# A second level of Strassen for layer 0 of a two-layer graph network, with a new order rule for VectorE and GpSimd

## The chip, the core and the metric

The kernel runs on one core of one Trainium2 chip. The time is the device time of one execution in microseconds (us), and a figure for a kernel is the median of its executions. Kernels are compared by their ratio to the kernel before.

Engines in the profile: PE is TensorE's matmuls, PEld its weight loads, DVE VectorE, ACT ScalarE, POOL GpSimd, SP the queue that issues transfers.

## The reference

```
x: 128 graphs x 128 nodes x 512 features; adj: 128 x 128 x 128; all float32
# layer 0
deg = sum(adj, -1);  agg = (adj @ x) / max(deg, 1e-6)
u = layernorm(x + relu(concat[x, agg] @ W0.T))
# layer 1: three graph convolutions
h1 = relu(adj @ (u @ W1) + b1);  h2 = relu(adj @ (h1 @ W2) + b2)
out = layernorm(u + adj @ (h2 @ W3) + b3)
```

Layer 0 is computed as x @ Wa + (adj / deg) @ (x @ Wb). So there are five weight products (y = x Wb, l0 = x Wa, and h1, s2, s3) and four adjacency products.

## The kernel before

Four graphs are one quad, and there are 32 quads. A weight product is a 512x512 by 512x512 product cut into 2x2 blocks of 256x256, and Strassen's method in Winograd's form makes it seven block products in place of eight. One block product is four matmuls of 128x128 weights by 256 columns:

```python
def product(p, a, b, k, start, transposed):
    (ta, ka), (tb, kb) = a.block(k), b.block(k)
    def emit():
        for o in range(2):
            for c in range(2):
                ...                                   # lhsT 128x128, rhs 128x256
                pinned(nc.tensor.matmul(bank_ap(p)[:, o, :], lhsT, rhs, start=..., stop=c == 1))
    plan.op("PE", 1.728, emit, ka + kb, [p])
```

Partial sums stay in a PSUM bank as long as possible. Where an intermediate sum is wanted, ScalarE copies the bank to SBUF and TensorE adds the next product to the same bank (`py` below):

```python
def wino_a(key, a, b, c00, c11, transposed=False, inner=None):
    py, pz, px = Slot("bank"), Slot("bank"), Slot("bank")
    product(py, a, b, 1, True, transposed)
    s1 = copied(py)                                   # ScalarE: bank -> SBUF
    product(pz, a, b, 5, True, transposed)
    product(py, a, b, 6, False, transposed)           # adds to py once s1 is taken
    s2 = copied(py)
    product(px, a, b, 2, True, transposed)
    ...
```

The sums of blocks that Strassen wants are made by GpSimd for the data and by VectorE for the weights (once). Each quad's degrees are summed by VectorE, inverted, written to HBM and read back so that every partition has the row:

```python
def degrees(q):                       # abridged
    vector(..., nc.vector.tensor_reduce(d, AR_T[q % 2], axis=AX.X, op=OP.add))   # "deg"
    ...
    dma(dd <- d)       # 2 KB, element by element
    dma(R_T <- dd)     # read back as a row for all partitions
```

All instructions are first put into a plan. A small list scheduler with a duration for each operation fixes the order of every engine before anything is emitted; TensorE may take an operation from up to `AHEAD = 24` places further on if the first one is not ready. Two quads are always in flight: layer 0 and h1 of one, and s2, h2, s3 and the last product of the one before it.

## Time and profile before

| | before |
|---|---|
| median time | 2423.27 us (2419.84 to 2429.75, 4 runs) |
| profiled span | 2426.3 us |
| TensorE busy | 2390.6 us, 11776 records |
| VectorE / ScalarE / GpSimd busy | 864.1 / 800.6 / 895.2 us |

TensorE is the bound, without a hole in whole periods. The prediction below shows the lines, so only the reading is given here: look first at the share of TensorE in the span and in the chain that ended last, then at the periods, and only then at its few waits. A busy engine's mean duration is not its pace, because matmuls are pipelined; the pace is the distance between starts.

### The profile page before, as it was taken

How to read it: one execution, taken by the hardware profiler on the slowest of the kernel's cores; microseconds unless marked ns; L12 is line 12 of the kernel's file. 1: busy time of each engine (PE TensorE's matmuls, PEld its weight loads, DVE VectorE, ACT ScalarE, POOL GpSimd, SP SyncE). 2: the span in 40 equal slices, each digit the busy share in tenths (PEclk: the TensorE clock that was granted, in tenths of full speed). 3: DMA queues.
4: the chain of work that ended last, by engine and by line, in shares of the span. 5: the costliest groups of instructions: out<-in, count | busy, mean ns of one | idle time of the engine just before them, and what ended most of it. 6: DMA issues, size and time to landing. Idle time of an engine off the chain costs nothing.

```text
span 2426.3 us, 29271 instructions
## 1 busy us (share of the span) xinstructions
PE 2390.6 (99%) x11776; PEld 2079.8 (86%) x11776; DVE 864.1 (36%) x1685; ACT 800.6 (33%) x1345; POOL 895.2 (37%) x772
## 2 busy tenths in 40 slices
PE   7999999999999999999999999999999999999997
PEld 6888888888888888888888888888888888888886
DVE  5433332333333333332343333333323433233323
ACT  2233333233332333233333333333233333333333
POOL 3333433334333344332443333433334432344323
PEclk9999999999999999999999999999999999999999
DMA  8201211112111121110111111211111111011100
GB/s 208 57 30 63 66 49 57 44 48 65 53 56 48 40 65 57 53 61 27 65 57 53 61 41 51 66 57 53 51 37 61 53 48 61 22 61 55 42 18 35
DMA packets 56360, 133.30 MB, mean 55 GB/s; under 512 B 21920, under 2 KB 27040, under 8 KB 48160
## 3 DMA queue, kind: packets, MB, share of 16 engines
q1 hardware_dynamic: 55552, 131.16, 16.9%
q8 instruction: 93, 1.52, 0.3%
q14 instruction: 43, 0.35, 0.1%
q10 hardware_dynamic: 672, 0.26, 0.1%
HBM read 97.78 MB, written 33.62 MB: 54 GB/s over the span
## 4 chain that ended last, share of the span: by engine, by line
PE 95%; DMA 3%; DVE 1%; issue 0%; ACT 0%; SPq 0%; POOL 0%; ACTq 0%; POOLq 0%; DVEq 0%
PE bank L408 77%; PE bank L646 5%; PE bank L687 5%; PE bank L421 4%; PE bank L563 4%; DMA dd<-deg 2%; DMA r<-dd 1%; DMA xT<-in_xT_dram 0%; DVE st L489 0%; SPq L265 0%; DVE deg L374 0%; DVE ah L275 0%; DVE row L275 0%; DVE deg L375 0%; ACT s L394 0%
## 5 line engine op out<-in xcount | busy, mean ns | idle before, releaser
L273 POOL TENSOR_TENSOR T<-T 128x512 f32<-128x512 f32 x384 | 484.9, 1274 | 1225.0 <-ACT T L656 970.1
L408 PE MATMUL bank<-w,T 128*128 128x256 f32 x3584 | 800.1, 379 | 2.3 <-ACT s L394 2.3
L408 PEld LDWEIGHTS bank<-w,T 128*128 128x128 f32 x3584 | 675.9, 190 | 92.8 <-ACT s L394 2.3
L394 ACT COPY s<-bank 128x512 f32<-128x512 f32 x480 | 281.3, 586 | 1225.5 <-PE bank L408 1225.2
L275 DVE TENSOR_TENSOR row<-bank,s 128x512 f32<-128x512 f32 x288 | 198.8, 691 | 690.5 <-PE bank L408 545.3
L408 PE MATMUL bank<-wb,xT 128*128 128x256 f32 x1792 | 404.5, 380 | 6.0 <-DMA wb<-in_w0T_dram 5.6
L408 PEld LDWEIGHTS bank<-T,w 128*128 128x128 f32 x1792 | 340.3, 190 | 74.5 <-issue 31.3
L408 PE MATMUL bank<-T,w 128*128 128x256 f32 x1792 | 397.8, 379 | 1.5 <-issue 1.5
L408 PE MATMUL bank<-wa,xT 128*128 128x256 f32 x1792 | 397.7, 379 | 0.0
L408 PEld LDWEIGHTS bank<-wb,xT 128*128 128x128 f32 x1792 | 341.5, 191 | 53.3 <-issue 5.6
L408 PEld LDWEIGHTS bank<-wa,xT 128*128 128x128 f32 x1792 | 340.5, 190 | 46.3
L273 POOL TENSOR_TENSOR u<-u,b 128x512 f32<-128x512 f32 x128 | 164.3, 1285 | 188.0 <-PE bank L563 186.4
L273 POOL TENSOR_TENSOR xT<-xT 128x512 f32<-128x512 f32 x128 | 163.8, 1280 | 61.6 <-DMA xT<-in_xT_dram 49.4
L563 PEld LDWEIGHTS bank<-at,u 128*128 128x128 f32 x1024 | 130.9, 195 | 12.4 <-ACT u L506 6.8
L563 PE MATMUL bank<-at,u 128*128 128x128 f32 x1024 | 132.3, 279 | 6.4 <-ACT u L506 6.4
L275 DVE TENSOR_TENSOR bank<-bank,s 128x512 f32<-128x512 f32 x96 | 67.2, 700 | 195.3 <-PE bank L421 195.3
L421 PE MATMUL bank<-row,ah 128*128 128x256 f32 x512 | 126.2, 379 | 2.3 <-DVE ah L275 2.3
L687 PE MATMUL bank<-row,at 128*128 128x512 f32 x256 | 120.5, 594 | 5.6 <-DVE row L275 5.6
L646 PEld LDWEIGHTS bank<-at,row 128*128 128x128 f32 x1024 | 119.4, 192 | 1.7
L530 DVE SCALAR_TENSOR_TENSOR u<-bank,x 128x512 f32<-128x512 f32 x128 | 88.3, 690 | 89.7 <-PE bank L421 87.5
L590 ACT ACTIVATE T<-T,b 128x256 f32<-128x256 f32 x192 | 90.5, 503 | 89.0 <-DVE T L275 89.0
L646 PE MATMUL bank<-at,row 128*128 128x128 f32 x1024 | 119.5, 275 | 0.0
(30 smaller groups left out, 1226.1 us busy)
## 6 DMA issues: line engine op xcount, KB each, us to landing
x<-in_x_dram SPq DMA_DIRECT2D x32, 1024.0 KB, 6.5
out_dram<-o SPq DMA_DIRECT2D x64, 512.0 KB, 2.6
xT<-in_xT_dram SPq DMA_DIRECT2D x31, 1024.0 KB, 4.8
ar<-in_adj_dram SPq DMA_DIRECT2D x32, 256.0 KB, 2.8
at<-in_adjT_dram SPq DMA_DIRECT2D x32, 256.0 KB, 2.6
r<-dd SPq DMA_DIRECT2D x31, 256.0 KB, 4.5
w<-in_w_dram SPq DMA_DIRECT2D x12, 256.0 KB, 10.1
xT<-in_xT_dram SPq DMA_DIRECT2D x4, 256.0 KB, 5.0
```

What stands on the lines that cost most here:

```text
L273: gpsimd(n, lambda: pinned(nc.gpsimd.tensor_tensor(dst(), a(), b(), op=op)), reads, writes)
L275: vector(n, lambda: pinned(nc.vector.tensor_tensor(dst(), a(), b(), op=op)), reads, writes, shared)
L394: scalar(512, lambda: pinned(nc.scalar.copy(S_T[s.index], bank_ap(p))), [p], [s])
L408: nc.tensor.matmul(bank_ap(p)[:, o, :], lhsT, rhs, start=start and o == 0 and c == 0, stop=c == 1, skip_group_check=True,)
L421: nc.tensor.matmul(bank_ap(p)[:, j, :], AH_T[:, g, :], y.t[:, g, h * H : (h + 1) * H], start=False, stop=True, skip_group_check=True,)
L530: nc.vector.scalar_tensor_tensor(u.ap(m, h), bank_ap(p), 0.0, X.ap(m, h), op0=OP.max, op1=OP.add)
L563: nc.tensor.matmul(bank_ap(p)[:, c // 2, (c % 2) * P : (c % 2 + 1) * P], u.t[:, g, c * P : (c + 1) * P], a[:, g, :], start=True, stop=True ...
L590: lambda t=t, o=o: pinned(nc.scalar.activation(t, t, AF.Relu, bias=B1_T[:, 2 * h + o : 2 * h + o + 1])),
L646: nc.tensor.matmul(bank_ap(p)[:, g // 2, (g % 2) * P : (g % 2 + 1) * P], s.t[:, g, o * P : (o + 1) * P], a[:, g, :], start=True, stop=True ...
L687: nc.tensor.matmul(bank_ap(p).rearrange("p a n -> p (a n)"), a[:, g, :], s.t[:, g, :], start=True, stop=True, skip_group_check=True,)
```

## The change

The intent: in y and l0, all quads but the first cut each of the seven 256x256 block products again, into seven products of 128x128 blocks. That makes 49 matmuls of 128 columns where 28 of 256 columns stood. It needs inner sums of the weights (once) and of xT (each quad). The first four outer products are summed before the last three are added. Around it, the scheduler's rules change: VectorE may take a sum planned for GpSimd when that sum is urgent (`HELP`), the search ahead is longer, and a GpSimd instruction that is planned behind a VectorE instruction on their common port waits for it by semaphore (`behind`). The deadlines of the work behind TensorE are reckoned anew (`HOLD`). Buffers are rearranged to make room, the degree row is loaded straight into the tile of the scaled adjacency, and s3's end has an order of its own. Smaller parts ride along: the adjacency is loaded and its degrees summed at another place in the plan, xT is loaded and the output stored in twice as many transfers, and the layer norm's epsilon is added on GpSimd.

The diff, cut to its core ("..." marks cuts):

```diff
-    AHEAD = 24
+    AHEAD, HELP, HOLD = 32, 8.0, 8.0
...
             if o.shared:
-                port = (o.engine, end)
+                if o.engine == "POOL" and port[0] == "DVE":
+                    o.behind = port[2]
+                port = (o.engine, end, o)
...
+                if e == "DVE":
+                    can += [
+                        o for o in known["POOL"]
+                        if o.other and ready_at[o] <= t and o.latest + slip < t + self.HELP and has_room(o, t)
+                        and port_free(e, t)
+                    ]
...
+    def inner_product(p, a, b, ps, i, start):
+        parts = [(a.inner(k, i), b.inner(k, i)) for k in ps]
+        def emit():
+            for n, ((ta, _), (tb, _)) in enumerate(parts):
+                pinned(nc.tensor.matmul(quarters(p, 4)[:, n], ta, tb, ...))      # 128 columns each
+        plan.op("PE", 0.222 * len(ps), emit, ...)
+
+    def outer_a(key, a, b, c11):              # outer products 1, 7, 6, 5: batch of four
+        inner_product(py, a, b, BATCH[0], 1, True)
+        s1 = copied(py)
+        inner_product(pz, a, b, BATCH[0], 5, True)
+        inner_product(py, a, b, BATCH[0], 6, False)
+        ...
+        add("POOL", F, outer(2), outer(2), outer(0), ...)
+        add("POOL", F, outer(1), outer(1), outer(2), ...)
+        c11(outer(1), outer(3), ...)
+        add("POOL", F, outer(2), outer(2), outer(3), ...)
+
+    def outer_b(key, a, b, sink, inner=None): # outer products 2, 4, 3: batch of three
+        inner_product(py, a, b, BATCH[1], 1, True)
+        s1 = over(0, 0)                       # VectorE: bank + sum of the first batch -> SBUF
+        ...
...
     for o in plan.order():
-        o.emit()
+        o.ins = o.emit()
+        if o.behind is not None:
+            tc.add_manual_dep(o.ins.ins, o.behind.ins.ins.name, ...)
```

## The prediction

> **What bounds the kernel now.** I read the page first, then the chain that ended last, the windows of one period each, the timeline of TensorE, and the waits. From the page:
>
> ```profile
> span 2426.3 us, 29271 instructions
> PE 2390.6 (99%) x11776; PEld 2079.8 (86%) x11776; DVE 864.1 (36%) x1685; ACT 800.6 (33%) x1345; POOL 895.2 (37%) x772
> PE 95%; DMA 3%; DVE 1%; issue 0%; ACT 0%; SPq 0%; POOL 0%; ACTq 0%; POOLq 0%; DVEq 0%
> ```
>
> TensorE is busy 99% and holds 95% of the chain; no other engine is above 37%. Only 35.7 us (2426.3 − 2390.6) of the span is without a matmul. So the time is the sum of the matmuls plus those 35.7 us, and a change gains only if it shortens the matmul stream without opening new holes in it.
>
> The windows view, three consecutive stretches of one period (74.47 us, a quad of four graphs) from the middle:
>
> ```profile
> 1241.40:1315.90 74.50, 74.50 (x370) 64.92 (x369) 27.03 (x52) 25.03 (x44) 27.84 (x24) 1.00 0.17 54
> 1315.90:1390.40 74.50, 74.50 (x370) 64.91 (x369) 26.10 (x52) 25.03 (x44) 27.84 (x24) 1.00 0.15 53
> 1390.40:1464.80 74.40, 74.40 (x370) 64.82 (x369) 26.92 (x52) 24.93 (x43) 27.84 (x24) 1.00 0.16 54
> ```
>
> The columns are stretch, length, then busy time of PE, weight loads, VectorE, ScalarE, GpSimd, the clock and DMA. TensorE has no hole at all; VectorE and GpSimd work 26 to 28 us of 74.5. The clock is 1.00.
>
> The timeline of TensorE gives the pace by shape, start to start, which the mean durations (379 and 275 ns) do not:
>
> ```profile
> 238.45 8.80 PE L408 MATMUL bank<-wa,xT 128*128 128x256 f32 x40
> 247.08 1.03 PE L421 MATMUL bank<-row,ah 128*128 128x256 f32 x4
> 247.94 3.73 PE L646 MATMUL bank<-at,row 128*128 128x128 f32 x32
> 251.51 1.03 PE L421 MATMUL bank<-row,ah 128*128 128x256 f32 x4
> ```
>
> One matmul of the program is two records (3584 + 3 x 1792 = 8960 records of L408 in 32 quads are 280 a quad, for 35 products of four matmuls). Forty records of 256 columns take 247.08 − 238.45 = 8.63 us, 0.2158 each: 0.4315 us for a program matmul. Thirty-two of 128 columns take 251.51 − 247.94 = 3.57 us, 0.1116 each: 0.223 us. Half the columns cost 51.7% of the time.
>
> The waits of TensorE add to little:
>
> ```profile
> PE bank L563 <- ACT u L506: 6.4, 1, 6.4
> PE bank L408 <- DMA wb<-in_w0T_dram: 5.6, 1, 5.6
> PE bank L687 <- DVE row L275: 5.6, 3, 2.8
> PE bank L408 <- ACT s L394: 2.3, 3, 0.8
> PE bank L421 <- DVE ah L275: 2.3, 1, 2.3
> ```
>
> The first, second and last belong to the first quad; the fourth to the last quad, which has nothing to run beside it; the third is three mid-run stalls behind VectorE. After the last matmul come some 11.7 us of layer norm and output. VectorE is in order, and its degree sum waits for a small strided transfer in 28 of 32 quads:
>
> ```profile
> DVE deg L374 <- DMA dd<-deg: 124.7, 28, 7.7
> ...
> dd<-deg SPq DMA_DIRECT2D x31, 2.0 KB, 8.6
> ```
>
> (waits view, then the DMA view.) That is 4.5 us each, which TensorE felt only three times. The kernel's scheduling table assumes about 3.8 us for it (2.0 + 400000/0.22e6, from its code), against 8.6.
>
> **What the Trainium skill says.** "TensorE: Matmul & The Clock Gate", section Back-to-back issue gap, says that weight load and matmul together set the pace, so small N costs more than its columns. The trace agrees mildly: 111.6 against 215.8 ns per record. "Perfetto Trace Analysis", section Matmuls, warns that "Larger matmuls are more efficient than smaller matmuls, when possible"; here the penalty is 3.4% on the 128-column form, which must be paid out of Strassen's 12.5%. "SBUF — State Buffer", section Who interferes with whom, says that a VectorE instruction with two SBUF inputs shuts out a GpSimd instruction that reads SBUF and the other way round. The trace agrees: 128x512 sums on VectorE take 691 ns with one input in PSUM and 1232 ns for the weight sums w<-w, SBUF only, made while GpSimd works. "GPSIMD Engine Reference", section 3.1, has GpSimd 1.96 times slower than VectorE on a tensor_tensor of 2048 elements; here it is 1274 against 691 ns, 1.84.
>
> **The change part by part, TensorE first.** Layer 0 has two weight products per quad (y and l0). Each is now 7 products x 4 matmuls x 256 columns. With the second level it is 7 x 7 = 49 matmuls of 128 columns.
> - Before: 28 x 0.4315 = 12.08 us. After: 49 x 0.223 = 10.93 us. Gain 1.15 us, twice per quad: 2.31 us.
> - Aggregation: before 8 x 0.4315 = 3.45 us. After, one block stays at 256 columns (2 x 0.4315) and three are cut in quarters (12 x 0.223): 3.54 us. Loss 0.09 us.
> - Net 2.22 us per quad, 31 quads (the first keeps one level): 68.8 us. Record counts rise by 31 x (2 x 42 + 12) = 2976, to 14752.
>
> That is the gain if no hole opens: 2423.3 − 68.8 = 2354.5 us.
>
> **GpSimd.** It gains eight inner sums of xT per quad (four of 512 elements at 1.27 us, four of 384 at about 0.97: 9.0 us), eight sums that combine the first batch's blocks (four per product, 10.2 us) and the small epsilon adds. 27.8 becomes about 48 us of a 72.3 us period, two thirds. The helper rule hands some to VectorE. Over the run: 895 + 31 x 19.2 + the epsilon adds, about 1500 us if none moves. That is off the critical path as a sum; what counts is where its chains lie.
>
> **VectorE.** Counted from the code, y goes from three bank sums to three full ones plus seven of 384 columns, and l0 from eight full operations to five plus twelve of 384 (an estimate of 0.53 us each, by scaling). That is about +8 us, near 34 of 72 us. ScalarE gains about one copy.
>
> **Where the chains lie.** The longest is xT: the next quad's transposed rows come only after l0 has read the last ones. Between the end of l0 and the next y, TensorE has s3 (12.1), g1 (3.6), the last products (3.4) and h1 (12.1), together 31 us. In it must fit a load of 4.8 us, four xT sums (5.1), the inner sums (9.0) and the four g1 sums (5.1), which are wanted first: 24 us. It fits, with 7 us over. Second, the combine chain of l0: bank sum 0.7, two or three GpSimd sums of 1.27, then the first subtraction from a bank, about 5 to 6 us with hand-over; TensorE has h2 (3.6), one aggregation (0.9) and two to four independent inner products (0.9 to 0.7 each) for that. Just enough. Third, the short accumulations: a bank's copy to SBUF takes 0.59 us plus hand-over on both sides, near 0.95, and a group of four inner matmuls is 0.89, of three 0.67. The former product gave 1.73. So TensorE must find other work at each such copy; the search ahead (now 32) is for that.
>
> **First and last quad.** The first quad's l0 now puts a sixth product ahead of the first aggregation, which should take most of the 2.3 us wait there. Against it, quad 1 needs 14 us of xT sums on GpSimd and 16 inner weight sums on VectorE (about 10 us, both on the common port), just where the trace shows w<-w already stretched; TensorE has only h1 of quad 0 (12 us) until they are ready. I choose +5 us for the start. At the end, s3's product 3 taken early should save about 1 us of the 2.3 us ScalarE waits.
>
> **The wait on VectorE** in itself costs nothing I can find: GpSimd would have been shut out by the port for that time anyway, and it fixes the order that was planned.
>
> Sum: 2354.5 + 5 (start) − 2.7 (first and last quad) + 2 (new small mid-run stalls beyond the 5.6 us that exist) = 2359 us, −2.7%.
>
> **Rivals.**
> - Holes in the steady stream: if each second-level group leaves 0.3 us at some six hand-overs per quad, that is 1.8 us x 31 = 56 us, and the time is about 2410. For it: 0.95 against 0.67 to 0.89 above. Against it: before, with the same planner, whole periods show 74.50 of 74.50 busy, so its model of TensorE, ScalarE and GpSimd is good to within a hand-over.
> - In-order VectorE held up by the degree transfer now reaches TensorE more often, since combine chains pass through VectorE: 1.5 us in half of the quads gives +23 us, about 2380. For it: 28 waits of 4.5 us exist. Against: the wait falls in the s3/g1 part, not in l0's chain.
> - GpSimd becomes the bound through the port: it would need above 72 us per period. 48 us plus a few of blocking does not reach it. Unlikely.
> - A cleaner result: no start-up cost and the mid-run stalls gone: 2347.
>
> **Range and chances.** The arithmetic gain is firm because both paces are read from the same trace; only holes can take from it. Low end 2345, high end 2385 (second rival in full plus some of the first). Two per cent is at 2374.8, so holes of 20 us beyond the arithmetic would spoil the verdict: faster 0.85, same 0.14, slower 0.01.
>
> **What would show it.** Records of TensorE 14752; the 128-column groups at 0.112 us start to start; periods of about 72.25 us; TensorE's idle total near 40 us; GpSimd near 1400 to 1500 us busy and VectorE near 1100. The prediction is wrong if the 128-column pace with xT weights is slower than 0.112, if periods exceed 73 us by waits of TensorE on VectorE, ScalarE or GpSimd in y or l0, or if the start before the second quad grows by over 10 us.

## More of the kernel before

The kernel before was run beside every experiment. Its time depends on the chip: 2423 us where the change was first measured, 2432 to 2434 us on the three chips of the experiments.

## The result, and the profile after

| | before | after |
|---|---|---|
| median time | 2423.27 us | 2359.56 us (2356.37 to 2361.43, 4 runs) |
| profiled span | 2426.3 us | 2359.6 us |
| ratio | 1 | 0.9733 (95% interval 0.971 to 0.9756) |

A ratio here is the mean time of one kernel's fast runs over that of the other's in the same rounds, so it is not quite the ratio of the medians. The change makes the kernel 2.7% faster, and the predicted 2359 us is within 1 us. The working shows below that this closeness is partly luck.

In the lines below, xT is the transposed x of a quad and xI its inner sums, w, wa and wb are weights (wa_i, wb_i their inner sums), T is layer 1's data, v holds the sums of the first batch, s are scratch tiles, at and ah the adjacency and its scaled form, deg and dd the degrees in SBUF and HBM. L503 is the 256-column product, L533 the inner product, L303 and L305 are sums on VectorE and GpSimd.

The page of the changed kernel (span, busy times, chain by engine):

```profile
span 2359.6 us, 36581 instructions
PE 2331.4 (99%) x14752; PEld 2116.4 (90%) x14752; DVE 1259.8 (53%) x2418; ACT 809.0 (34%) x1376; POOL 1096.6 (46%) x1080
PE 93%; DMA 4%; DVE 1%; ACT 0%; issue 0%; SPq 0%; POOL 0%; POOLq 0%; ACTq 0%; DVEq 0%
```

TensorE still bounds it, with exactly the 14752 records predicted. VectorE rose by 396 us and GpSimd by only 201 us. With every sum left to GpSimd it would have risen by 595 us (1490.3 in experiment 3), so two thirds of that work went to VectorE under the helper rule.

Two stretches of 72.2 us from the windows view, with columns as in the prediction (stretch, length, PE, weight loads, VectorE, ScalarE, GpSimd, clock, DMA):

```profile
1291.00:1363.20 72.20, 72.20 (x471) 66.00 (x470) 36.16 (x68) 23.25 (x40) 38.47 (x38) 1.00 0.15 49
1363.20:1435.40 72.20, 71.95 (x457) 65.22 (x456) 39.96 (x79) 26.99 (x46) 32.01 (x32) 1.00 0.18 56
```

The stream is still dense, but no longer wholly so. Periods alternate between two orders, so that GpSimd has 38 us in one and 32 in the next. From one quad's g1 to the next it is 73.1 us and about 71.9 us in turn, 72.5 us in the mean of the middle.

The timeline of TensorE in l0 of one quad:

```profile
164.89 1.06 PE L533 MATMUL bank<-wa,xI 128*128 128x128 f32 x8
165.78 1.06 PE L533 MATMUL bank<-wa,xT 128*128 128x128 f32 x8
166.67 1.06 PE L533 MATMUL bank<-wa_i,xI 128*128 128x128 f32 x8
167.57 1.95 PE L898 MATMUL bank<-at,row 128*128 128x128 f32 x16
```

Eight records of the new form take 165.78 − 164.89 = 0.89 us, 0.111 us each, the pace that the prediction took from the adjacency products. The fourth line is h2's product, drawn in between two groups of l0: the search ahead at work.

The waits of TensorE:

```profile
PE bank L814 <- ACT u L711: 7.2, 7, 5.2
PE bank L503 <- DMA wb<-in_w0T_dram: 5.7, 1, 5.7
PE bank L533 <- DVE s L303: 3.7, 1, 3.7
```

The third is new: one wait of 3.7 us. It stands at 80 us, and experiment 4 finds its cause. **A ledger** makes the two traces comparable. Every start of a matmul that came more than 30 ns later than the pace of its form counts as a pause. Pauses and the stretch behind the last start then add up with the matmuls' own time to the span (all in us, worked out from the start times):

| | before | after | difference |
|---|---|---|---|
| matmuls at their pace (0.216, 0.112, 0.429 us a record) | 2382.6 | 2314.8 | −67.8 |
| first matmul | 5.6 | 5.7 | 0 |
| pauses up to 58 us (quad 0, slow clock included) | 14.6 | 13.1 | −1.5 |
| pauses from 58 to 100 us (quad 1 starts) | 1.7 | 6.6 | +4.9 |
| pauses in the middle | 6.4 | 7.0 | +0.6 |
| pauses of the last quad | 3.1 | 3.7 | +0.6 |
| from the last matmul's start to the end | 12.3 | 8.9 | −3.4 |
| span | 2426.3 | 2359.6 | −66.6 |

The end got shorter, and the timelines put it down to the order; no experiment takes that order out by itself. Before, all four graphs' layer norms stood behind the last matmuls; now s3's block product 3 comes before 4, two graphs are finished early, and two remain. The timeline at the end, before:

```profile
2415.25 2.46 DVE L489 BATCH_NORM_STATS2 st<-o 128x6 f32<-128x512 f32 x4
```

and after:

```profile
2347.78 1.28 DVE L694 BATCH_NORM_STATS2 st<-s 128x6 f32<-128x512 f32 x2
...
2352.02 1.28 DVE L694 BATCH_NORM_STATS2 st<-s 128x6 f32<-128x512 f32 x2
```

The pair at 2347.78 runs beside matmuls (the last one starts at 2350.8); before, the four started together at 2415.25, after the last matmul's start at 2414.0.

### The profile page after: what moved, and what is told of

Its sections match the earlier page's. It is cut to its first block, busy times and chain, and to the rows that moved or that the text cites.

```text
span 2359.6 us, 36581 instructions
## 1 busy us (share of the span) xinstructions
PE 2331.4 (99%) x14752; PEld 2116.4 (90%) x14752; DVE 1259.8 (53%) x2418; ACT 809.0 (34%) x1376; POOL 1096.6 (46%) x1080
## 4 chain that ended last, share of the span: by engine, by line
PE 93%; DMA 4%; DVE 1%; ACT 0%; issue 0%; SPq 0%; POOL 0%; POOLq 0%; ACTq 0%; DVEq 0%
PE bank L503 48%; PE bank L533 27%; PE bank L898 5%; PE bank L814 5%; DMA dd<-deg 4%; PE bank L935 4%; PE bank L546 4%; PE bank L515 1%; DMA ar<-in_adj_dram 0%; DVE st L694 0%; ACT u L711 0%; DVE row L303 0%; DMA wb<-in_w0T_dram 0%; DVE u L751 0%; DVE v L303 0%
## 5 line engine op out<-in xcount | busy, mean ns | idle before, releaser
L503 PE MATMUL bank<-w,T 128*128 128x256 f32 x3584 | 815.2, 380 | 1.2 <-ACT s L489 0.7
L503 PEld LDWEIGHTS bank<-w,T 128*128 128x128 f32 x3584 | 665.1, 191 | 83.9 <-ACT s L489 1.1
L305 POOL TENSOR_TENSOR T<-T 128x512 f32<-128x512 f32 x248 | 311.6, 1275 | 375.3 <-ACT T L908 272.8
L503 PE MATMUL bank<-T,w 128*128 128x256 f32 x1792 | 403.5, 380 | 0.7 <-ACT s L489 0.7
L503 PEld LDWEIGHTS bank<-T,w 128*128 128x128 f32 x1792 | 334.3, 190 | 44.7 <-ACT s L489 1.1
L303 DVE TENSOR_TENSOR v<-bank,s 128x512 f32<-128x512 f32 x186 | 128.2, 689 | 306.3 <-PE bank L533 202.7
L303 DVE TENSOR_TENSOR row<-bank,s 128x512 f32<-128x512 f32 (+1 forms) x288 | 183.7, 646 | 180.6 <-PE bank L503 158.1
L305 POOL TENSOR_TENSOR xT<-xT 128x512 f32<-128x512 f32 x183 | 222.8, 1228 | 42.3 <-DMA xT<-in_xT_dram 15.3
L305 POOL TENSOR_TENSOR s<-v 128x512 f32<-128x512 f32 x31 | 39.4, 1270 | 419.0 <-DVE v L303 369.5
L303 DVE TENSOR_TENSOR s<-bank,v 128x384 f32<-128x384 f32 x186 | 103.7, 558 | 144.1 <-PE bank L533 132.9
L303 DVE TENSOR_TENSOR T<-bank,s 128x512 f32<-128x512 f32 x96 | 66.2, 690 | 189.9 <-PE bank L503 97.5
L305 POOL TENSOR_TENSOR u<-u,b 128x512 f32<-128x512 f32 x128 | 160.1, 1281 | 11.1 <-DVE T L303 5.1
L303 DVE TENSOR_TENSOR T<-T 128x512 f32<-128x512 f32 x136 | 97.8, 725 | 50.4 <-ACT T L824 36.6
L303 DVE TENSOR_TENSOR v<-v 128x512 f32<-128x512 f32 x169 | 116.7, 691 | 9.9 <-POOL v L305 1.7
L533 PEld LDWEIGHTS bank<-wb,xT 128*128 128x128 f32 x868 | 110.5, 192 | 8.8 <-issue 7.2
```

What stands on the lines that cost most here:

```text
L303: on_vector = lambda: pinned(nc.vector.tensor_tensor(dst(), a(), b(), op=op))
L305: on_gpsimd = lambda: pinned(nc.gpsimd.tensor_tensor(dst(), a(), b(), op=op))
L503: nc.tensor.matmul(bank_ap(p)[:, o, :], lhsT, rhs, start=start and o == 0 and c == 0, stop=c == 1, skip_group_check=True,)
L533: nc.tensor.matmul(quarters(p, 4)[:, n], ta, tb, start=start and n == 0, stop=True, skip_group_check=True)
```

## The experiments

The theory that the prediction implies (A): the gain is matmul columns, and everything else is small. The rivals: the new rules carry a good part (B), the chains of sums only fit because of the helper rule (C), and the new hole at 80 us has one of two causes (D). Each edit is against the changed kernel unless it says otherwise. All results were correct.

**1. One level in every quad (e1_one_level).** This takes the second level out and keeps every rule, buffer and ordering of the change.

```diff
 def seg_y_a(q):
-    if q == 0:
+    if q >= 0:
         return wino_a(("y", q), XA, WB, ...)
 ... (y_b likewise; l0: one level, its first half placed where outer_a stood)
-            XA.inner_sums()        # nor WB.inner_sums(), WA.inner_sums()
```

> The changed kernel with layer 0 at one level of Strassen in every quad and no inner sums; its scheduling rules, its wait of GpSimd on VectorE, its buffers and its ending all stay. Theory A (the gain is matmul columns: 67.8 us by the start-to-start paces of the two traces): the 67.8 us come back, and what the second level cost in holes goes (6.6 us in quad 1, some 7 us of small ones in the middle), so about 2410 to 2420 us, 0.995 to 0.999 of the kernel before. Rival B (the new scheduling rules and the port wait carry a good part): under 2400 us.

Measured: 2413.55 us against 2434.28 us for the kernel before, ratio 0.991 (0.9888 to 0.9931). In time it lies in theory A's band, but that band was reckoned from the 2423 us of another chip; as a ratio, which is the fair measure, it is just below. So all of the change but the second level is worth 0.9%, some 21 us, more than the prediction's 2.7 us. In its ledger (span 2411.1) the pauses are 14.6 us in place of 25.9 (the kernel before's trace, from another chip), of which 0.1 in the middle, and the end is 8.5 us. The changed kernel is at 0.9733 to 0.9737, so the second level itself brought 1.7%, about 42 us, and not the 67.8 us of its columns. The difference is pauses that it opened: 37.1 us of them in experiment 5's trace.

**2. Without GpSimd's wait for VectorE (e2_no_port_wait).**

```diff
-        if o.behind is not None:
+        if False and o.behind is not None:
             tc.add_manual_dep(...)
```

> The changed kernel without the semaphore by which GpSimd waits for VectorE; the planned order is the same. Theory A: the port makes GpSimd wait anyway, so 2360 us within 5 us. Rival B: the wait is needed for the order of the two engines at their port, and without it GpSimd gets in first and VectorE stands blocked, with new holes of TensorE: over 2370 us.

Measured: 2387.41 us, ratio 0.9803 (0.9781 to 0.9824). Against the changed kernel's 0.9737 in experiment 5 that is 0.66%, 16 us, lost, and the order of every engine is the same instruction for instruction. Theory A fell. The timeline shows how. In the changed kernel, VectorE:

```profile
176.15 0.69 DVE L303 TENSOR_TENSOR T<-T 128x512 f32<-128x512 f32 x1
176.75 0.68 DVE L303 TENSOR_TENSOR v<-v 128x512 f32<-128x512 f32 x1
177.53 0.56 DVE L303 TENSOR_TENSOR s<-bank,v 128x384 f32<-128x384 f32 x1
```

and GpSimd in the same place:

```profile
177.57 1.27 POOL L305 TENSOR_TENSOR s<-v 128x512 f32<-128x512 f32 x1 [3.31 <-issue]
```

GpSimd starts when VectorE's sum v<-v is through. (The view names no releaser for its 3.31 us of idle time; that it is the semaphore follows from the edit.) Without the semaphore, VectorE:

```profile
177.21 0.68 DVE L303 TENSOR_TENSOR T<-T 128x512 f32<-128x512 f32 x1
177.81 1.75 DVE L303 TENSOR_TENSOR v<-v 128x512 f32<-128x512 f32 x1
179.66 0.56 DVE L303 TENSOR_TENSOR s<-bank,v 128x384 f32<-128x384 f32 x1
```

GpSimd:

```profile
177.42 1.59 POOL L305 TENSOR_TENSOR s<-v 128x512 f32<-128x512 f32 x1 [2.10 <-PE bank L533]
```

and TensorE behind it:

```profile
180.27 0.94 PE L533 MATMUL bank<-wa_i,xI 128*128 128x128 f32 x6 [0.34 <-DVE s L303]
```

GpSimd gets in at 177.42, while VectorE is still at T<-T. The next VectorE sum, which is on the path to TensorE, then takes 1.75 us in place of 0.68: GpSimd's sum ends at 179.01, and VectorE's at 179.56; that it stood at the port until then is read from these times. TensorE waits for what follows. The pauses in the middle are 31.2 us here against 7.0 in the changed kernel's first trace and 13.3 in its second.

**3. Without the helper rule (e3_no_help).** All sums planned for GpSimd stay there.

```diff
-    AHEAD, HELP, HOLD = 32, 8.0, 8.0
+    AHEAD, HELP, HOLD = 32, -1e9, 8.0
```

> The changed kernel with the rule off that hands GpSimd's sums to VectorE when they are near their deadline, so all stay on GpSimd. Theory A: GpSimd is busy about 1500 us (48 us of a 72 us period), its chains still fit behind TensorE's other work in the middle, and only the start gets longer: 2360 to 2375 us. Rival C: the chains only fit because VectorE, almost twice as fast, takes the urgent ones: TensorE waits on GpSimd in each quad and the time is over 2390 us.

Measured: 2408.2 us, ratio 0.9892 (0.9869 to 0.9914). GpSimd's busy time is 1490.3 us, which the prediction had worked out as about 1500, but the conclusion drawn from it was wrong: TensorE now waits for GpSimd in nearly every quad, as theory C says. From the waits of TensorE:

```profile
PE bank L503 <- POOL T L305: 38.0, 30, 3.1
```

That is 1.3 us each time, in 30 waits, on g1's sums, needed by h1. The pauses in the middle are 46.8 us. So with the second level but without this rule, nearly all is lost that the second level brings over experiment 1 (0.9892 against 0.991).

**4. The degree sum later (e6_degree_late).** The changed kernel has one big hole, 3.9 us at 80 us. VectorE's timeline before it:

```profile
70.80 0.69 DVE L303 TENSOR_TENSOR v<-bank,s 128x512 f32<-128x512 f32 x1 [1.66 <-ACT s L489]
78.72 0.69 DVE L469 TENSOR_REDUCE deg<-ar 128x4 f32<-128x512 f32 x1 [7.23 <-DMA ar<-in_adj_dram]
79.32 0.68 DVE L303 TENSOR_TENSOR v<-bank,s 128x512 f32<-128x512 f32 x1
```

VectorE stands for 7.23 us at the degree sum of a later quad, whose adjacency has not landed, and the sums of y stand behind it in the queue. The plan had let VectorE run far ahead: this is the fifth of the 32 degree sums, while TensorE is at y of the second quad. The adjacency was issued at 67.15 us, just after the small write of another quad's degrees at 66.58, and VectorE went on 11.6 us later; the median of all 32 such loads is 3.0 us. The edit makes the planned place later; it takes no wait away.

```diff
 def degrees(q):
+    after = row(q - 1, "y").keys() if q else []
...
-    ... tensor_reduce(d, AR_T, axis=AX.X, op=OP.add)), ["ar"], kd)
+    ... tensor_reduce(d, AR_T, axis=AX.X, op=OP.add)), ["ar"] + after, kd)
```

> The changed kernel with one more dependence in the plan: the degree sum of a quad comes after the previous quad's y, so VectorE, which is in order, no longer runs ahead into a late transfer. Theory D (the one big new hole, 3.9 us at 80 us and 2.7 us of slow clock after it, comes from VectorE standing at the degree sum of a later quad): that hole goes and some of the small ones too, 2348 to 2354 us. If the hole comes from the weights' inner sums instead, it stays: 2359 us.

Measured: 2351.54 us, ratio 0.9655 (0.9634 to 0.9676). The hole at 80 us is gone (no pause at all between 58 and 100 us), and the middle is down to 3.8 us. VectorE's waits at the degree sum, 58.5 us in the changed kernel's trace, are gone too, while the weights' inner sums stand at the same place within 2 us. So the cause is the degree sum, not the weights' inner sums. This version beats both kernels. Against experiment 1 on the same chip it is 62 us faster: with this hole out of the way the second level yields most of its 67.8 us.

**5. The changed kernel again (r_after), unaltered.**

> The changed kernel itself, unaltered, beside the kernel before on this chip. The kernel before took 2434 us on the chip of the first four experiments and 2423 us in the first result, so the ratio and not the time carries over: 0.973 within 0.003 if the changed kernel feels the chip's difference as the kernel before does; if the degree transfers are what differs between chips, the changed kernel moves less and the ratio is about 0.970.

Measured: 2368.71 us against 2432.47, ratio 0.9737 (0.9713 to 0.9762), the same as at first. In the ledger of its trace the hole at 80 us is 6.9 us with the slow clock behind it, and the middle has 13.3 us where the first trace had 7.0. So this kernel's time varies with the chip, in step with the kernel before. The trace shows where the added pauses lie: the 14 pauses of over 0.3 us in the middle, 9.7 of the 13.3 us, each begin 1.7 to 2.8 us after the start of a degree sum for which VectorE had waited 2.8 to 3.8 us, in every second quad. In the first trace there are six such pauses, 3.0 of the 7.0 us. VectorE's waits for the degree transfer add up to 64.6 us here and 49.6 us there, so the transfers are the likely way in which the chip counts; two traces do not show it, and the median time to landing of the degree write was no longer here (9.1 against 10.0 us). Experiment 4's version is 0.8% better by ratio, 0.9655 against 0.9737, and the intervals lie apart.

**6. One level without GpSimd's wait (e8_one_no_wait).** Experiments 1 and 2 together.

> One level of Strassen in every quad with the new rules, without GpSimd's wait for VectorE. With the wait this took 0.991 of the kernel before, 2413.6 us. Theory F (the wait is worth 27 us only because the second level puts sums of VectorE and GpSimd on TensorE's path): without it under 5 us more, at most 2419 us. If the wait pays by itself whatever the products, some 20 us more, 2434 us.

Measured: 2417.44 us, ratio 0.9937 (0.9912 to 0.9962), against 0.991 with the wait. The intervals overlap; the difference is some 7 us and not resolved, and the trace has no pause in the middle at all. The wait is thus worth about 16 us with two levels and little with one (the expectation's 27 us set times of two chips against each other; 16 is by ratio). Theory F holds.

**7. TensorE in written order, two levels (e4_strict_two).**

```diff
-    AHEAD, HELP, HOLD = 32, 8.0, 8.0
+    AHEAD, HELP, HOLD = 1, 8.0, 8.0
```

> The changed kernel with TensorE's order as written: the search ahead cut from 32 operations to 1. Theory A's step on short accumulations (a bank's copy takes about 0.95 us with both hand-overs, a group of four or three inner matmuls 0.89 or 0.67, so TensorE must find other work at each): 4 to 10 us of holes per quad, 2480 to 2670 us. If the hand-overs are hidden by the next group of the same product, it stays under 2400 us.

Measured: 2582.39 us, ratio 1.0614 (1.0574 to 1.0654), within theory A's band; but the band was meant for the short accumulations alone, and experiment 8 shows that they are only a part of it.

**8. TensorE in written order, one level (e5_strict_one).** The same edit on experiment 1's kernel.

> One level in every quad, with TensorE's order as written (no search ahead). With two levels this order took 2582 us, 214 us over the same kernel with the search (2369). Theory A (most of those holes belong to the second level's short groups, which one level's 1.73 us products cover): at most 70 us over the one-level kernel with the search, under 2485 us. If the written order is as bad for both (the layer norm before g1, the sums before s3), about 2580 to 2630 us.

Measured: 2474.34 us, ratio 1.017 (1.0132 to 1.0208). In written order, then, two levels are 108 us slower than one; with the search ahead they are faster. The waits of TensorE, two levels:

```profile
PE bank L814 <- ACT u L711: 49.1, 32, 4.7
PE bank L533 <- ACT s L489: 43.2, 62, 0.7
PE bank L503 <- POOL T L305: 26.7, 41, 1.5
PE bank L533 <- DVE s L303: 25.8, 32, 5.7
```

and one level:

```profile
PE bank L818 <- ACT u L711: 47.7, 32, 4.7
...
PE bank L503 <- ACT s L489: 4.0, 5, 1.3
```

The wait for the layer norm (first line of each) is common to both. The next line is the short accumulation: 62 waits of 0.7 us, two in each of 31 quads, for a bank's copy by ScalarE. In the timeline of two levels:

```profile
1033.50 1.16 PE L533 MATMUL bank<-wb_i,xT 128*128 128x128 f32 x8
1035.34 1.16 PE L533 MATMUL bank<-wb_i,xT 128*128 128x128 f32 x8 [0.68 <-ACT s L489]
```

Inner product 4 comes 1.84 us after 7, which is 0.95 us more than its group's 0.89: the hand-over that the prediction put at 0.95. But here 4 is written right behind 7 into the same bank, with nothing between; with one level, other products are written between the two, and there are five such waits in the whole run. Where one group of four stands between, as before 6 and 7, TensorE loses only 0.1 to 0.3 us. So the two runs differ in the written order as well as in the length of the groups, and the experiment does not part the two. The last two lines, 26.7 and 25.8 us, are waits for sums.

**9. Work for an idle TensorE (e9_warm).** On experiment 4's version, matmuls on zeros before the first data and in quad 0's wait for the layer norm. The Trainium skill, "TensorE: Matmul & The Clock Gate", section Part 1: The HAM clock gate (the "warmup" mystery), says that the clock is halved after a window of some 3.4 us without work. The traces agree for this pause: in 44 to 50 us, behind its 5.4 us, the granted clock is 0.58 in the changed kernel. For shorter pauses they do not bear the figure out: in experiment 10's trace a wait of 2.1 us at 1835 us was followed by 3.4 us at a clock of 0.51, while in the kernel before's trace one of 2.8 us at 575 us was followed by the full clock.

```diff
+    def warm(n): ...   # n matmuls of 256 columns on a zeroed tile into a bank of their own
+    warm(5)            # first of all
...
         if t == 0:
+            warm(9)
             WB.inner_sums()
```

> The version with the late degree sum, and beside it idle TensorE kept at work: five matmuls on zeros before the first data arrive, nine in the 5.4 us in which quad 0's layer norm is awaited. Theory E (a pause of TensorE[...] costs once more in a halved clock behind it: 5.1 us at the start and 2.4 us after quad 0 in that version's trace): up to 5 us come off the 2351.5 us of that version, and no more than 7. If the slow matmuls behind a pause are due to something else (weights not yet there, the port), nothing comes off.

Measured: 2351.02 us, ratio 0.9663 (0.9638 to 0.9688): no gain. The trace shows why it told little: nothing held the nine back, so the search ahead drew all fourteen matmuls to the front, and the first real product began at 9.26 us instead of 5.8. A failed experiment, mended in 11.

**10. The version of experiment 4 again (e12_late_again), as the measure for 11 and 12.**

> The version with the late degree sum once more, as the measure for the runs beside it on the same chip: 0.966 of the kernel before within 0.002, about 2351 us, with the hole at 80 us gone.

Measured: 2349.64 us, ratio 0.9662 (0.9636 to 0.9687), as expected.

**11. The same filling, held in its place (e11_warm_placed).**

```diff
+            warm(11, [("aggregated", 0, 0, 1)])   # waits for quad 0's last aggregation
```

> The version with the late degree sum, with matmuls on zeros before the first data (five) and, this time held back until the first quad's last aggregation, in the wait for the layer norm (eleven; before, the search ahead had drawn all fourteen to the front). Theory E: the matmuls of g1 then run at full clock, 2.4 us less than the version beside it, and the start gains at most 1 us, since the degrees bind it: 2 to 4 us less in the trace, at the edge of what the timing resolves.

Measured: 2352.63 us, ratio 0.9672 (0.9648 to 0.9696): no gain. The filling now works. The windows view of 44 to 50 us, in experiment 4's version:

```profile
44.00:50.00 6.00, 5.53 (x29) 5.53 (x30) 4.28 (x9) 3.41 (x6) 0.91 (x2) 0.57 0.81 150
```

and here:

```profile
44.00:50.00 6.00, 5.08 (x30) 4.32 (x29) 5.12 (x14) 2.41 (x4) 2.16 (x4) 1.00 0.69 115
```

(The third figure from the end is the clock: 1.00 here against 0.57 there.) But what the clock gave, the start took: TensorE reached the first aggregation early, at 29.3 us, and waited 4.5 us for the scaled adjacency, which came at 33.8 us:

```profile
33.81 2.91 PE L516 MATMUL bank<-row,ah 128*128 128x256 f32 x8 [4.47 <-DVE ah L303]
```

The degrees bind the first quad, and faster matmuls ahead of them only lengthen that wait. That is not the whole of it: the sum that makes the scaled adjacency began at 33.1 us here and at 31.2 us in experiment 10's trace, for a reason that was not looked for, and g1, which still waits for the layer norm, starts at 48.3 us in place of 44.3.

**12. Two levels in the first quad too (e10_first_two).** On experiment 4's version, with the inner sums of the weights and of xT moved to the front.

```diff
-        if q == 0:          # one level in the first quad
+        if q < 0:
 ...
     XA.sums()
     WB.sums()
+    XA.inner_sums()
+    WB.inner_sums()
```

> The version with the late degree sum, with two levels in the first quad too. Its matmuls take 2.2 us less. Theory G (the start is bound by what has to be summed before the first inner products: 16 weight sums on VectorE at 0.55 to 0.68 us and 12 xT sums): VectorE's sums lengthen the start by 5 to 15 us, so 3 to 13 us over the version beside it. If the start is bound by the degree transfers alone (the scaled adjacency is ready at 30 to 32 us in every version), the sums hide in that wait and it is the same within 3 us.

Measured: 2372.28 us, ratio 0.9748 (0.9723 to 0.9773), 22.6 us slower than experiment 10 on the same chip. The two traces are 15.4 us apart, since the run profiled in experiment 10 was the slowest of its four and the one here the fastest. The direction is theory G's, the size is not: the first matmul begins at 9.0 us in place of 5.7, and g1 of quad 0 at 62.9 in place of 44.3. TensorE waits for sums, and its short groups with gaps between them also run at the slow clock; the pauses up to 58 us rise from 13.3 to 28.5 us. So leaving the first quad at one level is worth 15 to 23 us, where its matmuls cost 2.2.

## Why the prediction was right, and where it was not

**The columns.** Right: −68.8 us predicted, −67.8 in the ledger, with the predicted record count and pace. The mean period, 72.5 us, is near the predicted 72.25.

**The pauses.** The sum was right (+4.3 predicted for start, first and last quad and middle; +4.5 in the ledger), but its terms were not what they were taken for, and that they added up is luck. Experiment 1 shows two larger effects that nearly cancel. The rest of the change took pauses of 25.9 us down to 14.6, and the end from 12.3 to 8.5. The second level then put pauses back, to 30.4 us in the first trace and 37.1 in the second. The prediction had the rules at −2.7 us and the second level at +7. Which of its parts took the old pauses away was not separated. The sign "TensorE's idle total near 40 us" failed by the page, which shows 28.2 us (2359.6 − 2331.4); in the ledger start, pauses and end are 45.0. The page hides short pauses: a record of 256 columns counts as busy for 0.38 us, while the next can start after 0.216.

**The start of quad 1.** "I choose +5 us for the start" met the measured +4.9, for another reason. The prediction blamed the weights' inner sums on VectorE; experiment 4 removed the hole without touching them. It is the in-order VectorE at a degree sum whose data are late. That the size fitted is luck.

**"The wait on VectorE in itself costs nothing I can find: GpSimd would have been shut out by the port for that time anyway".** This step failed. The first half, no cost, stands; the reason behind it was wrong, and the benefit was missed. GpSimd is not shut out if it comes first, and then it is VectorE, on the way to TensorE, that stands. Experiment 2 puts the wait's worth at about 16 us, a quarter of the gain.

**GpSimd's chains.** "It fits, with 7 us over" failed as well for GpSimd alone. The estimate of its work was right (about 1500 us, 1490 measured), but 48 us of work in a 72 us period still left TensorE waiting 1.3 us a quad in experiment 3. The fit of the kernel as it is comes from the helper rule, which the prediction mentioned and did not count; it therefore had GpSimd too high (1400 to 1500 us; 1097) and VectorE too low (1100; 1260).

**The short accumulations.** The hand-over was right (0.95 us measured in experiment 8), and the search ahead does cover it: in the changed kernel's waits view no product of the second level waits for such a copy. How much it would cost uncovered is open: in written order the copies took 43.2 us and the waits for sums 52.5 us, and the written order was part of both.

**The rivals.** Holes in the steady stream, at 2410, did not come about; experiment 3, at 2408.2, has their size from another cause, GpSimd's sums. The in-order VectorE at the degree transfer was put at 1.5 us in half of the quads, 23 us in all. It was real: moving the degree sum gave 0.8%, about 20 us on chips where the changed kernel takes 2369, of which the hole at 80 us and what followed it are 6.9, and in the middle of experiment 5's trace it is indeed every second quad, at 0.3 to 1.3 us. The argument against it, that the wait falls in the s3/g1 part and not in l0's chain, did not hold at 80 us, where sums of y stood behind it. The end's −3.4 us was foreseen by no step: the prediction expected 1 us less of waits from s3's new order, and the pauses of the last quad grew by 0.6 instead.

**Open.** Of the 13.3 us in the middle of the second trace, 9.7 lie behind waits at the degree sum; what the other 3.6 us of small pauses come from, and whether the two-quad alternation has a part in either, was not tried apart from experiment 4.

## What to carry to other kernels

Count columns and pace for the gain, but look for what holds the pauses down: here the search ahead and the helper rule decide whether a second level of Strassen pays, and the semaphore brings a quarter of the gain. When two engines share a port, ask in which order they come to it; a semaphore that makes the non-urgent one wait can be worth it. On an engine that works in order, never place an instruction that waits for a slow transfer earlier than it is needed.

## What the Trainium skill lacked or had wrong

- "SBUF — State Buffer", section Who interferes with whom, is right that the order of issue decides who blocks, and experiment 2 agrees: VectorE's 0.68 us sum became 1.75 us when GpSimd was first. The page names no means to fix the order: a semaphore that does was worth 16 us of 2369 here.
- "TensorE: Matmul & The Clock Gate", section Back-to-back issue gap, gives no pace for float32. Here a float32 matmul is two records; a record is 0.216 us at 256 columns and 0.112 us at 128, with a new 128x128 weight load for each hidden behind it.
- "DMA: Bandwidth & Descriptors", section Latency and other measured facts, speaks of a fixed cost of about 2 us and has no latency for a small scattered write. Here 2 KB of degrees, written element by element, landed a median 8.6 us (before) and 10.0 us (after) from issue, with any time in the queue.
